# Moving the edge features' products of the last attention into the first four attention loops

## The chip, the cores and the metric

The kernel runs on one core of a Trainium2 chip. The core has five engines with a queue of instructions each: TensorE (PE: matrix products and transposes), VectorE (DVE), ScalarE (ACT), GpSimd (POOL) and SyncE (SP, which issues DMAs). Sixteen DMA engines move data between HBM and the on-chip memories. The metric is the time of one execution on the device, in microseconds; a shorter time is better.

## The reference

The program is a graph network on 3125 nodes with 256 numbers each and 50,000 edges, sorted by destination. Four attention layers over the edges alternate with four feed-forward layers, each added to x after a normalisation:

```
x = x + L0_gnn(norm(x))   # attention, 8 heads of 32
x = x + L0_ffn(norm(x))   # 16 experts, 2 per token
x = x + L1_gnn(norm(x))   # attention
x = x + L1_ffn(norm(x))   # 8 experts, 2 for the batch
x = x + L2_gnn(norm(x))   # two attentions, one after the other
x = x + L2_ffn(norm(x))   # an attention over 65,536 other edges gives the gates; 4 dense experts
x = x + L3_gnn(norm(x))   # attention with edge features
x = x + L3_ffn(norm(x))   # 8 dense experts
```

The last attention is the only one that uses the features of the edges, an input of 50,000 x 256 numbers:

```
e     = (edge_attr @ We).reshape(-1, 8, 32)
kj    = k[src] + e
alpha = sum(q[dst] * kj) / sqrt(32)          # then a softmax over the edges of one destination
out   = segment_sum((v[src] + e) * alpha)
```

The product `edge_attr @ We` depends on inputs alone, so it can be made at any time before the last attention. All arithmetic is in float32.

## The kernel before

The edges are laid out as 128 partitions of T = 391 consecutive edges; the last 48 places are padding. An attention runs over groups of GW = 8 columns of edges (8 x 128 edges), 49 groups in all. The stages follow each other: `gnn0`, `ffn0`, `gnn1`, `ffn1`, `gnn2` (two attentions, g2a and g2b), `ffn2`, `gnn3`, `ffn3`.

The first four attentions (g0, g1, g2a, g2b) share `gat_once`. One group is: eight gathers by GpSimd (`gather`, L129), each of which fetches 128 rows of 272 numbers into one of four buffers `hg`; the logits on VectorE (L607, L534); `weigh` (L624 on), where VectorE makes running maxima, ScalarE the exponential (L652) and a copy of the maxima (L653), and VectorE the weighted running sums (L660, L668); and a store of the group, 1088 KB, by SyncE (L611). TensorE has nothing to do in these loops, apart from the transposes of a sort (L338) which is laid into the first sixteen groups of g0. After the loop, `join_chunks` (L713) joins the chains that cross partitions. It begins with a gather of rows that were just stored (`fixrow`).

`ffn2` has a loop of its own, eight groups of GB = 64 gathers of 128 rows of 24 numbers (L1380). Into the first five groups it lays the 28 pieces of its experts' work on TensorE and ScalarE (`expert`, L1348; six pieces a group), whose results go to HBM in stores of 512 KB (L1370). In each of the eight groups it also calls `copy_features` (L952): one DMA that copies an eighth of the edge features, 6.2 MB, from the input to a second place in HBM called `attr`.

`gnn3` reads `attr`, never the input. When the given edges were not sorted, an `If` at its start (L838) fills `attr` in the order of the sort by gathers; with the given inputs this body is jumped over. The loop of gnn3 (L919) has 49 groups too, with sixteen gathers each: eight rows of 520 numbers (`kv`, three buffers) and eight rows of 256 (`q`). `project` (L894) runs two pairs of columns ahead of VectorE: it loads eight columns of `attr` (1 MB, L902), TensorE transposes a pair (L907, four transposes), ScalarE copies the result (L909), and TensorE multiplies it by We (L913). VectorE adds the product to k and v and multiplies by q (L930, L932, L933), sums over each head (L937) and goes on as in `weigh`.

In the attention loops and in that of ffn2 the order of VectorE and ScalarE is that of the program (`manual_schedule`). Elsewhere, and on the other engines, a scheduler orders the instructions when the program is built. Each engine works its queue in order.

Of the kernel before, what the change touches and what calls it, by code (L numbers as in the profile page):

```python
# [19 lines left out]
P = 128  # L20
# [18 lines left out]
class Kernel:  # L39
# [514 lines left out]
    def gat_once(self, L, tag, load_z, load_w, a_src, a_dst, H, dh, eps, loops, use):  # L554
# [11 lines left out]
        with tc.tile_pool(name=tag + "k", bufs=1) as kp:  # L566
# [25 lines left out]
            with tc.tile_pool(name=tag + "e", bufs=1) as sp, tc.tile_pool(name=tag + "v", bufs=4) as vp, \  # L592
# [7 lines left out]
                for t in range(0, T, GW):  # L600
# [10 lines left out]
                    nc.sync.dma_start(out=rows[:, t : t + n, :], in_=g[:, :n, :])  # L611
                nc.vector.tensor_copy(R, carry[0])
# [11 lines left out]
    def weigh(self, L, carry, vp, pp, t, n, l, g, H, dh):  # L624
# [32 lines left out]
        for j0 in range(0, n, GV):  # L657
            k = min(GV, n - j0)
            v = pp.tile([P, GV, W], F32, name="v")
# [167 lines left out]
    def gnn3(self, L):  # L827

        nc, tc, a, T, Ep = self.nc, self.tc, self.a, L.T, L.Ep
# [3 lines left out]
        Q = self.dram.tile([NP, C], F32, name="g3_Q")  # L833
        KV = self.dram.tile([NP, C + W], F32, name="g3_KV")
        OUT = self.dram.tile([Ep + 1 + P, RW], F32, name="g3_OUT")
        heads = lambda x: x.rearrange("p n (h d) -> p n h d", h=H)
        r = nc.values_load(L.wrong[0:1, 0:1], min_val=0, max_val=P)
        with tc.If(r > 0):  # L838
            with tc.tile_pool(name="g3s", bufs=3) as sp:
                rows = self.attr.rearrange("(p t) c -> p t c", p=P)  # L840
                for t in range(T):
                    x = sp.tile([P, C], F32, name="ax")
                    self.gather(x, a["edge_attr_256"], L.tab[:, t, 2:3])
                    nc.sync.dma_start(out=rows[:, t, :], in_=x)
# [37 lines left out]
        with tc.tile_pool(name="g3k", bufs=1) as kp:  # L882
            R = kp.tile([P, W], F32, name="R")
            mR = kp.tile([P, H], F32, name="mR")
            we = kp.tile([P, KC, C], F32, name="we")
            nc.sync.dma_start(out=we, in_=a["L3_gnn_We"].rearrange("(k p) f -> p k f", p=P))
            attr = self.attr.rearrange("(p t) c -> p t c", p=P)
            rows = OUT[:Ep].rearrange("(p t) w -> p t w", p=P)
            with tc.tile_pool(name="g3v", bufs=3) as vp, tc.tile_pool(name="g3vp", bufs=1, space=PSUM) as pp, \
# [4 lines left out]
                def project(i):  # L894
# [5 lines left out]
                    if j == 0:  # L900
                        at[t] = vp.tile([P, GW, C], F32, name="at", bufs=2)
                        nc.sync.dma_start(out=at[t][:, :n, :], in_=attr[:, t : t + n, :])  # L902
                    k2 = min(2, n - j)
                    pt = pp.tile([P, 2, KC, P], F32, name="apt")
# [6 lines left out]
                    for i2 in range(k2):  # L911
                        for k in range(KC):
                            nc.tensor.matmul(pe[:, i2, :], aT[:, i2, k, :], we[:, k, :], start=(k == 0), stop=(k == KC - 1))  # L913
                    proj[i] = pe

                project(0)
                project(1)
                carry, i = None, 0
                for t in range(0, T, GW):  # L919
# [6 lines left out]
                    for j in range(0, n, 2):  # L926
# [7 lines left out]
                        project(i + 2)  # L934
# [9 lines left out]
            self.join_chunks(L, "g3", OUT, R, mR, H, dh)  # L944
# [5 lines left out]
            self.node_results(L, "g3", OUT, H, dh, 1e-16, None, use)  # L950

    def copy_features(self, E, i, n):  # L952
# [596 lines left out]
```

## Time and profile before

| what | value |
|---|---|
| three timed runs | 7157.77, 7183.26 and 7185.37 us, median 7183.26 us |
| the profiled execution, its own time | 6277.97 us |
| its span, first to last instruction | 6275.9 us |
| mean granted clock of TensorE | 0.677 |
| busy shares of the span | PE 41%, DVE 56%, ACT 13%, POOL 51% |
| moved by DMA | 963.74 MB |
| loop of g0, first gather to last VectorE result | 148.4 to 666.1 us |
| loop of g1 | 1436.7 to 1940.5 us |
| loop of g2a | 2321.4 to 2824.7 us |
| loop of g2b | 2937.2 to 3438.7 us |
| loop of ffn2 | 3575.0 to 4342.8 us |
| loop of gnn3 | 4556.4 to 5577.2 us |

Times inside the program are microseconds from the start of the span. The profiled execution is shorter than the timed runs by some 900 us, and nothing on the page tells why; times of stages are of the profiled execution. A row of instructions reads: line, engine, operation, what it writes and reads, how often; then busy time and mean nanoseconds of one; then the idle time of the engine just before such instructions, with what ended most of it. "issue" is time in which an engine waited for nothing that the profile shows.

### The profile page before, as it was taken

What the parts mean: (1) busy time and instruction counts of PE and PEld (TensorE: products, weight loads), DVE (VectorE), ACT (ScalarE), POOL (GpSimd) and SP (SyncE); (2) the same over time, 40 slices, a digit from 0 to 9 for tenths busy, and PEclk for the clock granted to TensorE, in tenths of its full rate; (3) what the DMA queues carried; (4) which work ended last, traced back from release to release, by engine and by line L of the source; (5) the groups of instructions that cost most, each with busy time, mean ns of one, the idle gap of its engine ahead of it and who ended that gap; (6) DMA issues with size and microseconds to landing.
All of it is one profiled execution on the core that took longest, in us unless ns stands there. A gap on an engine that the chain in (4) does not pass through costs nothing. (4 is left out here: it accounts for less than half of the span.)

```text
span 6275.9 us, 39477 instructions
## 1 busy us (share of the span) xinstructions
PE 2584.4 (41%) x9265; PEld 1734.2 (28%) x9265; DVE 3504.1 (56%) x8011; ACT 794.9 (13%) x1810; POOL 3231.9 (51%) x3326
## 2 busy tenths in 40 slices
PE   2000049920001940002000499400566666639999
PEld 1000037710000530001000355200244555525555
DVE  6998611156886268884777411112778888871111
ACT  1000012210001110001000122100011111102222
POOL 3777430037774137775776576675077777730000
PEclk9555569955555975555555699755777666657999
DMA  5566335416663026663666234522377888730000
GB/s 193 191 225 221 124 115 169 156 57 197 223 219 109 14 64 224 220 218 109 212 212 204 52 109 123 154 55 67 144 256 262 264 268 262 264 123 16 10 11 26
DMA packets 398594, 963.74 MB, mean 154 GB/s; under 512 B 92478, under 2 KB 241053, under 8 KB 365966
## 3 DMA queue, kind: packets, MB, share of 16 engines
q1 hardware_dynamic: 236254, 538.71, 23.9%
q0 software_dynamic: 162096, 422.40, 23.2%
q8 instruction: 77, 1.26, 0.1%
q14 instruction: 167, 1.37, 0.1%
HBM read 611.38 MB, written 400.71 MB: 161 GB/s over the span
## 5 line engine op out<-in xcount | busy, mean ns | idle before, releaser
L724 PE MATMUL mRT<-ident,mR 128*8 128x128 f32 (+2 forms) x6 | 2.2, 372 | 2230.5 <-DVE mR L613 1356.0
L129 POOL DMA_INDIRECT hg<-g_H,A_tab x782 | 758.1, 969 | 240.4 <-issue 225.0
L668 DVE SCALAR_TENSOR_TENSOR hg<-hg,A_keep,v 128x264 f32<-128x264 f32 (+1 forms) x1368 | 666.2, 487 | 44.2
L129 POOL DMA_INDIRECT hg<-f_H,B_tab x512 | 519.3, 1014 | 232.9 <-issue 148.2
L724 PEld LDWEIGHTS mRT<-ident,mR 128*8 128x8 f32 (+2 forms) x6 | 0.5, 82 | 2233.1 <-issue 2233.1
L913 PE MATMUL ape<-we,aT 128*128 128x256 f32 x1564 | 493.6, 487 | 150.9 <-DVE kv L932 147.3
L129 POOL DMA_INDIRECT kv<-g_KV,A_tab x391 | 370.9, 949 | 295.3 <-issue 279.3
L660 DVE TENSOR_TENSOR v<-hg,e 128x1056 f32<-128x1056 f32 (+1 forms) x392 | 488.0, 1245 | 3.6 <-ACT e L652 3.6
L913 PEld LDWEIGHTS ape<-we,aT 128*128 128x128 f32 x1564 | 384.3, 252 | 251.1 <-DVE kv L932 164.4
L129 POOL DMA_INDIRECT hg<-g2a_H,A_tab x391 | 372.8, 953 | 119.2 <-issue 106.7
L129 POOL DMA_INDIRECT hg<-g2b_H,A_tab x391 | 371.5, 950 | 119.2 <-issue 114.0
L129 POOL DMA_INDIRECT q<-g_Q,A_tab x391 | 370.8, 948 | 120.1 <-issue 105.2
L1386 DVE TENSOR_TENSOR l<-hg,ad 128x256 f32<-128x256 f32 x8 | 6.3, 790 | 632.0 <-DMA hg<-f_H,B_tab 632.0
L1501 DVE SCALAR_TENSOR_TENSOR xs<-ps,g,xs 128x256 f32<-128x256 f32 x200 | 94.2, 484 | 458.1 <-PE ps L1500 458.1
L652 ACT ACTIVATE e<-d 128x72 f32<-128x72 f32 (+1 forms) x245 | 54.8, 223 | 2141.0 <-DVE d L649 2141.0
L125 PE MATMUL tr<-ident,z 128*128 128x128 f32 x450 | 109.5, 374 | 498.2 <-DVE z L117 434.6
L134 POOL DMA_INDIRECT A_Z<-D,A_first x100 | 99.3, 993 | 356.1 <-PE hps L584 223.4
L907 PE MATMUL apt<-ident,at 128*128 128x128 f32 x782 | 193.1, 382 | 196.6 <-ACT aT L909 188.2
L129 POOL DMA_INDIRECT y<-f_Y,pos x50 | 47.5, 949 | 398.3 <-DMA f_Y<-y 383.4
L125 PEld LDWEIGHTS tr<-ident,z 128*128 128x128 f32 x450 | 71.6, 200 | 535.1 <-ACT ln_rs L109 316.6
L1494 ACT ACTIVATE hT<-ps,bn 128x512 f32<-128x512 f32 (+1 forms) x224 | 162.4, 731 | 390.5 <-PE ps L1492 390.5
L930 DVE TENSOR_TENSOR kj<-kv,ape 128x512 f32<-128x512 f32 x196 | 135.9, 693 | 132.3 <-PE ape L913 112.1
(476 smaller groups left out, 6471.9 us busy)
## 6 DMA issues: line engine op xcount, KB each, us to landing
g_OUT<-hg SPq DMA_DIRECT2D x96, 1088.0 KB, 5.0
g2a_OUT<-hg SPq DMA_DIRECT2D x48, 1088.0 KB, 4.9
g_OUT<-kv SPq DMA_DIRECT2D x48, 1088.0 KB, 6.4
g2b_OUT<-hg SPq DMA_DIRECT2D x48, 1032.0 KB, 4.6
at<-attr SPq DMA_DIRECT2D x48, 1024.0 KB, 4.9
w<-in_L_ffn_w_dram SPq DMA_DIRECT2D x80, 512.0 KB, 3.9
attr<-in_edge_attr_dram SPq DMA_DIRECT2D x5, 6256.0 KB, 25.7
attr<-in_edge_attr_dram SPq DMA_DIRECT2D x3, 6240.0 KB, 26.9
```

Of the source, the lines that this page charges most:

```text
L125: nc.tensor.transpose(ps[:, k, :], z[:, t, k * P : (k + 1) * P], self.ident)
L129: return self.nc.gpsimd.indirect_dma_start(out=out, out_offset=None, in_=table, in_offset=bass.IndirectOffsetOnAxis(ap=idx, axis=0))
L134: i = self.nc.gpsimd.indirect_dma_start(out=table, out_offset=bass.IndirectOffsetOnAxis(ap=idx, axis=0), in_=in_, in_offset=None)
L652: nc.scalar.activation(e, d, AF.Exp)
L660: nc.vector.tensor_tensor(vals(v)[:, :k], vals(g[:, j0 : j0 + k, :W]), e[:, :, j0 + 1 : j0 + k + 1].rearrange("p h n -> p n h").unsqueeze( ...
L668: nc.vector.scalar_tensor_tensor(to, prev, L.keep[:, t + j0 + j : t + j0 + j + 1], v[:, j, :], op0=ALU.mult, op1=ALU.add)
L907: nc.tensor.transpose(pt[:, i2, k, :], at[t][:, j + i2, k * P : (k + 1) * P], self.ident)
L913: nc.tensor.matmul(pe[:, i2, :], aT[:, i2, k, :], we[:, k, :], start=(k == 0), stop=(k == KC - 1))
L930: nc.vector.tensor_tensor(kj[:, :k2], g[:, j : j + k2, :C], pe[:, :k2], ALU.add)
L1386: nc.vector.tensor_tensor(ln, g[:, :, W:].rearrange("p n h -> p h n"), ad[:, t : t + GB, :H].rearrange("p n h -> p h n"), ALU.add)
L1494: nc.scalar.activation(hT[:, f, :n], ps[:, :n], AF.Relu, bias=bn[l][1][:, c0 : c0 + 1], scale=bn[l][0][:, c0 : c0 + 1])
L1501: nc.vector.scalar_tensor_tensor(self.xs[:, t, :], po, g[:, t, e : e + 1], self.xs[:, t, :], op0=ALU.mult, op1=ALU.add)
```

## The change

The copy of the features is gone. Instead a new function `features` is called once in every group of the first four attention loops, 4 x 49 = 196 times, for a pair of columns each time. It is a pipeline of three steps, of which each call advances every pair in flight by one. One call copies the product of the pair before the last out of PSUM and stores it (256 KB to `attr`), copies the last pair's transposes out of PSUM and multiplies them by We, transposes a pair that was loaded at the call before, and loads the next pair (256 KB, two columns of each of the 128 partitions). `end_features` empties the pipeline after each loop. For the last 24 pairs, in g2b, where partition 127 has no edges left, a load is split into three or four DMAs. We is loaded once at the start and stays on chip. The tile `v` of `weigh` in PSUM has one buffer in place of two, to make room.

`attr` now holds products. In the last attention, `project` only loads eight columns and ScalarE copies them into PSUM, three pairs ahead; the transposes, copies and matrix products are gone. This goes for edges that came sorted, as here. For others the old way is kept, with gathers from the input in place of loads of `attr`. So the whole of `gnn3` is in the program twice, in the two arms of an `If`; the second arm is the one that runs here.

In ffn2, the experts' results are stored by two row blocks (256 KB, three buffers) and no longer by four (512 KB, two buffers).

```diff
                     carry = self.weigh(L, carry, vp, pp, t, n, l, g, H, dh)
                     nc.sync.dma_start(out=rows[:, t : t + n, :], in_=g[:, :n, :])
+                    self.features(vp, pp)
+                self.end_features(vp, pp)
...
-            v = pp.tile([P, GV, W], F32, name="v")
+            v = pp.tile([P, GV, W], F32, name="v", bufs=1)
...
+        r = self.nc.values_load(L.wrong[0:1, 0:1], min_val=0, max_val=P)
+        with self.tc.If(r > 0) as way:
+            self.gnn3_edges(L, False)
+        with way.Else():
+            self.gnn3_edges(L, True)
...
                     if j == 0:
                         at[t] = vp.tile([P, GW, C], F32, name="at", bufs=2)
-                        nc.sync.dma_start(out=at[t][:, :n, :], in_=attr[:, t : t + n, :])
+                        if ordered:
+                            nc.sync.dma_start(out=at[t][:, :n, :], in_=attr[:, t : t + n, :])
+                        else:
+                            for i2 in range(n):
+                                self.gather(at[t][:, i2, :], a["edge_attr_256"], L.tab[:, t + i2, 2:3])
                     k2 = min(2, n - j)
+                    if ordered:
+                        proj[i] = pp.tile([P, 2, C], F32, name="ape", bufs=3)
+                        nc.scalar.copy(proj[i][:, :k2], at[t][:, j : j + k2, :])
+                        return
...
+    def features(self, sp, pp, last=False):
+
+        nc, f = self.nc, self.feat
+        E, T = f["E"], f["T"]
...
+        loaded, turned, made = f["stages"]
+        if made is not None:
+            (t, n), pe = made
+            o = sp.tile([P, 2, C], F32, name="fe_o", bufs=2)
+            nc.scalar.copy(o[:, :n], pe[:, :n])
+            nc.sync.dma_start(out=rows[:, t : t + n, :], in_=o[:, :n])
+            made = None
+        if turned is not None:
+            (t, n), pt = turned
+            aT = sp.tile([P, 2, KC, P], F32, name="fe_T", bufs=2)
+            nc.scalar.copy(aT[:, :n], pt[:, :n])
+            pe = pp.tile([P, 2, C], F32, name="fe_p", bufs=1)
+            for i in range(n):
+                for k in range(KC):
+                    nc.tensor.matmul(pe[:, i, :], aT[:, i, k, :], self.feat_we[:, k, :], start=(k == 0), stop=(k == KC - 1))
+            made, turned = ((t, n), pe), None
+        if loaded is not None:
+            (t, n), at = loaded
+            pt = pp.tile([P, 2, KC, P], F32, name="fe_t", bufs=1)
+            for i in range(n):
+                for k in range(KC):
+                    nc.tensor.transpose(pt[:, i, k, :], at[:, i, k * P : (k + 1) * P], self.ident)
+            turned, loaded = ((t, n), pt), None
+        if not last and f["at"] < len(f["units"]):
+            t, n = f["units"][f["at"]]
+            f["at"] += 1
+            at = sp.tile([P, 2, C], F32, name="fe_a", bufs=3)
+            if full * T + t + n <= E:
+                whole = bass.AP(tensor=src.tensor, offset=src.offset + t * C, ap=[[T * C, P], [1, n * C]])
+                nc.sync.dma_start(out=at[:, :n, :].rearrange("p n c -> p (n c)"), in_=whole)
...
-                    y = wp.tile([P, 4, C], F32, name="y")
                     for i in range(n // P):
+                        if i % 2 == 0:
+                            y = wp.tile([P, 2, C], F32, name="y", bufs=3)
...
-                    self.copy_features(50000, i, T // GB)
```

## The prediction

> **What bounds the kernel now.** The page's busy shares name no bound: GpSimd 51%, VectorE 56%, TensorE 41%. So I cut the span at the loops and read busy time by stage; the rows below are g1, g2a, ffn2 and gnn3 (columns: stretch, its length, busy time of each engine, granted clock, DMA share, GB/s).
>
> ```profile
> 1438.00:1945.00 507.00, 1.80 (x5) 0.87 (x5) 406.12 (x850) 27.55 (x100) 373.38 (x392) 0.50 0.65 218
> 2321.00:2830.00 509.00, 1.97 (x5) 0.86 (x5) 406.55 (x850) 27.54 (x100) 374.72 (x394) 0.50 0.65 217
> 3575.00:4343.00 768.00, 412.48 (x1403) 244.63 (x1401) 113.31 (x247) 118.74 (x223) 519.30 (x512) 0.77 0.37 105
> 4556.00:5577.00 1021.00, 665.39 (x2346) 510.53 (x2346) 853.74 (x1372) 134.12 (x295) 741.69 (x782) 0.68 0.77 256
> ```
>
> In gnn3 VectorE looks like the bound (854 of 1021 us) and TensorE like the second. The groups of gathers say otherwise:
>
> ```profile
> L129 POOL DMA_INDIRECT hg<-f_H,B_tab x512 | 519.3, 1014 | 232.9 <-issue 148.2 <-DMA hg<-f_H,B_tab 84.7
> L129 POOL DMA_INDIRECT kv<-g_KV,A_tab x391 | 370.9, 949 | 295.3 <-issue 279.3 <-DMA kv<-g_KV,A_tab 4.3 <-DVE acc L656 3.7
> L129 POOL DMA_INDIRECT q<-g_Q,A_tab x391 | 370.8, 948 | 120.1 <-issue 105.2 <-DMA q<-g_Q,A_tab 4.9 <-DVE kv L668 2.1
> L129 POOL DMA_INDIRECT hg<-g2a_H,A_tab x391 | 372.8, 953 | 119.2 <-issue 106.7 <-DVE hg L668 12.5
> ```
>
> A gather takes 0.95 us, 0.30 us of issue precedes it, and it waits for next to nothing: 1.254 us from start to start. In gnn3 782 x 1.254 = 981 us, and from the first gather to the last there are 984. In g1, g2a, g2b 391 x 1.254 = 490 against 492 to 493. So GpSimd's issue sets all these loops; VectorE, TensorE and the DMAs run beneath it. Only ffn2 is off its floor: 512 x 1.254 = 642, and it takes 752. The timeline of GpSimd and SyncE there (start, duration, instruction, idle time before) shows why:
>
> ```profile
> 4042.17 3.44 POOL L129 DMA_INDIRECT hg<-f_H,B_tab  x1 [0.30 <-issue]
> ...
> 4052.51 0.56 SPq L960 DMA_DIRECT2D attr<-in_edge_attr_dram  x1
> ...
> 4064.40 0.95 POOL L129 DMA_INDIRECT hg<-f_H,B_tab  x1 [2.18 <-DMA hg<-f_H,B_tab]
> 4070.73 0.95 POOL L129 DMA_INDIRECT hg<-f_H,B_tab  x1 [5.38 <-DMA hg<-f_H,B_tab]
> 4076.65 0.94 POOL L129 DMA_INDIRECT hg<-f_H,B_tab  x1 [4.97 <-DMA hg<-f_H,B_tab]
> 4078.68 0.94 POOL L129 DMA_INDIRECT hg<-f_H,B_tab  x1 [1.08 <-DMA hg<-f_H,B_tab]
> ```
>
> After each copy of features (26 us to land) gathers wait for earlier gathers that are stuck behind it. A second loss is of another kind: some gathers are long themselves (3.44 us at 4042).
>
> **The change part by part**, against the profiled execution (6277.97 us).
>
> *The copy goes: -77 us.* The DMA waits are 84.7 us over 26 gathers, of which 26 x 0.3 is the usual issue: 77 remain, about 9.6 for each of eight copies. The long gathers stay. Of the whole excess of 110 us one would hope to get 110; [...] the 3.44 us gather lies under VectorE's 3.35 us multiply (L1405), the 2.40 us one under the 1.77 us copy (L1415). [...] I take 77, with 60 to 110 as ends. What could cover the gain: the experts. Six pieces take about 93 us of TensorE (28 in 435 us), a group of gathers would take 64 x 1.254 + 4 = 84. But the experts end with the fifth group at 3993, where the gathers of that group would then end too (3575 + 82 + 4 x 84.6 = 3995), and three buffers `hg` let GpSimd run ahead. So nothing is lost, barely. The smaller stores of y (256 KB) have 100 half-pieces of ScalarE to hide under: nothing.
>
> *The last attention's TensorE work goes: -24 us, all at its end.* 1564 matrix products of 487 ns, 782 transposes of 382 and 196 copies of 583 leave, and 196 copies from SBUF of the same shape come, some 0.58 us each, beneath VectorE. In the loop this is worth nothing: it lies under the 981 us of GpSimd. But VectorE, with 18 us of work and some 2 us of waits for `ape` in each 20 us, lags, and works off its last groups when the gathers are over:
>
> ```profile
> 5532.03 0.95 POOL L129 DMA_INDIRECT kv<-g_KV,A_tab  x1 [3.74 <-DVE acc L656]
> ...
> 5539.55 0.95 POOL L129 DMA_INDIRECT kv<-g_KV,A_tab  x1 [0.31 <-issue]
> ...
> 5543.50 0.70 DVE L930 TENSOR_TENSOR kj<-kv,ape 128x512 f32<-128x512 f32 x1 [1.30 <-PE ape L913]
> ...
> 5565.95 0.43 DVE L930 TENSOR_TENSOR kj<-kv,ape 128x256 f32<-128x256 f32 x1
> ...
> 5577.03 0.16 DVE L942 COPY mR<-m 128x8 f32<-128x8 f32 x1
> ```
>
> Without the waits VectorE (18.2 us) keeps up with GpSimd (20.06). The last gather lands 4.2 us after 5539.55, and from the last pair to mR there are 11.2 us: the end is at 5555 and not 5577, -22, and the 3.4 us wait at 5532 goes: I take -24 (-10 to -27). The bound itself is untouched.
>
> *gnn3 in an arm of an If: +7 us.* Before, the jump cost VectorE 1.02 us, over a body that held nothing for it. At the first If of the program VectorE jumps over some 1300 instructions:
>
> ```profile
> 41.04 0.42 DVE L191 CAST dstf<-A_tab 128x391 f32<-128x391 int32 x1 [4.28 <-DVEq L189]
> 4444.57 0.28 DVE L856 MEMSET none_row<- 1x272 f32 x1 [1.02 <-issue]
> ```
>
> The new jump is over as many, and the normalisation behind it is on the path. [...] by the nearer-looking row (1.02) the sum would gain nothing here, [...] I take 3.3. At the arm's end nothing of ffn3 can be ordered into gnn3's tail any more; before, the statistics of six of 25 tiles were (0.4 us each), [...] so +4 (0 to 10).
>
> *The features in four loops: +12 us.* Each group of 10.03 us gets four transposes (1.5 us by L907's row) and eight products (3.9 by L913's), on a TensorE that has 1.8 us of work in 507; two ScalarE copies of 0.58 on an engine with 27.5 us of work, placed after `weigh`, when VectorE has 6.6 us of sums to go; no instruction for VectorE or GpSimd. All that is hidden; if the cover were gone it would be the two copies in front of an exponential, 1.2 us a group. SyncE gets a load and a store a group, 512 KB: 196 x 512 KB = 100 MB, just the bytes of the copy that goes. A loop's rate rises by 25.7 MB / 507 us = 51 GB/s, from 218 to 269. The nearest row is gnn3, whose loop runs at 256 GB/s (the page's slices: up to 268): its 782 gathers wait 9.2 us for DMA in all, so 4.6 for 391. Four loops: 0 to 18, I take 8. The loads stand two groups ahead in SyncE's order, so they wait for nothing of their own group. The last pairs drain after the loop: a copy, four products and a copy, some 5 us after the last exponential, while `fixrow` waits 4.1 us for the last store anyway: 1 us a loop, +4 (0 to 12).
>
> *The sort in g0: +10 us.* In its first 16 groups VectorE is busy 175 of 185 us, and the sort's transposes now queue on TensorE behind the features' products, up to 4 us for each of 14. Slack after that doesn't come back, since GpSimd cannot catch up. 0 to 40; I take 10, near the bottom, since VectorE has the loop's own work between two steps of the sort. `v` with one buffer is written and read by VectorE alone, in order: nothing.
>
> Sum: -77 - 24 + 3 + 4 + 8 + 4 + 10 = -72 us, 6278 to 6206.
>
> **Against the median.** The timed runs are 7183 / 6278 = 1.144 times the profiled execution, and no row tells where the 905 us lie. If they lie outside the stages touched, the change is worth 72; if all is stretched alike, 82. I take 82: 7183 - 82 = 7101, forecast **7100 us** (its own range 7050 to 7145).
>
> **Rivals.**
> *The wait moves with the bytes.* The copy cost 77 us for 51 MB read and written. If a byte costs a gather as much in the four loops as in ffn2, 100 MB of loads and stores give 77 back, and with the 24 us of the tail and the 29 of other costs the sum is about +5: 7183 +- 25. For it: in ffn2 GpSimd stops some ten gathers after a burst. Against it: the group's own store of 1088 KB lands in 5.0 us without one DMA wait in g2a's row, and 256 KB more twice is a burst of some 2 us, not of 26.
> *The loops become bound by the stores, slower.* SyncE's queue and the 16 DMA engines have to pass 512 KB more in each 10.03 us; if `hg` comes free later than GpSimd needs it, each of 196 groups stretches. The row has the beginning of such a wait (12.5 us for `hg` in g2a). At 0.37 us a group the gain is used up, at 1 us it is +196 - 80 = +116, times 1.144: 7315. Against it: the DMA share of 0.65 would become about 0.8, which gnn3 bears.
> *gnn3's loop gets faster too*, if something other than issue sets the 1.254 us: its VectorE and TensorE suggest it, the row of waits speaks against it. 40 us more: 7055.
>
> **How the numbers follow.** The forecast 0.60, the bytes 0.20, the stores 0.13, the faster loop 0.07. Range 7035 to 7195: the low end is 110 for the copy and 26 for the tail, scaled; the high end has the sort at +40, the loops at +30 and half of the first gain. Half a percent (36 us) is about what a measurement of this kernel can tell from no change. Faster: 0.60 + 0.07 + a small part of the bytes, 0.68; same 0.19; slower 0.13.
>
> **What would show it.** Right: in ffn2 no gather waits for a DMA, and the loop takes about 690 us; gnn3's gathers still take 981 us, and mR follows the last one by about 15 us, not 37; the loops of g1 to g2b take 504 to 510 us. Wrong: DMA or `hg` waits in the rows of g1 to g2b, a g0 loop of over 550 us, or VectorE waiting over 5 us at the start of gnn3.

## The result and the profile after

The changed kernel takes 7232 us (15 runs, 7208 to 7250) against 7180 us for the kernel before in the same session (15 runs, 7158 to 7207): ratio 1.0067, 95% interval 1.0050 to 1.0084, so it is slower by two thirds of a percent. The forecast was 7100 us. The same program has two lengths, by session. The kernel before takes 6273 to 6282 us in four of the sessions below and 7124 to 7180 us in the other three and in that of the result; the profile shown before the prediction is of the first kind, its three timed runs of the second. They are called short and long sessions here. A session is a stretch of runs on one chip, with the kernel before and its variants in turn; comparisons are made within a session, or the text says that they are not.

The profile of the changed kernel is of the long kind (7250 us, span 7248.3). Its rows by stage, for g1, g2a, ffn2 and gnn3 (stretch, its length, busy time of PE, PEld, DVE, ACT, POOL, granted clock, DMA share, GB/s):

```profile
1571.00:2197.00 626.00, 196.45 (x571) 147.27 (x570) 406.12 (x844) 74.50 (x194) 372.66 (x392) 0.60 0.64 215
2580.00:3215.00 635.00, 199.22 (x570) 148.82 (x569) 406.22 (x844) 74.73 (x194) 373.76 (x393) 0.60 0.63 212
4094.00:5133.00 1039.00, 485.17 (x1434) 274.44 (x1432) 110.62 (x247) 120.59 (x226) 495.09 (x513) 0.70 0.12 28
5350.00:6547.00 1197.00, 0.37 (x1) 0.08 (x1) 859.89 (x1373) 142.17 (x295) 739.17 (x782) 0.50 0.66 218
```

The loops take 626 and 635 us where 507 and 509 were read before, with the same busy time of VectorE and GpSimd: all of the difference is idle. The groups of gathers say what GpSimd waited for:

```profile
L129 POOL DMA_INDIRECT hg<-f_H,B_tab x512 | 494.7, 966 | 527.8 <-DMA f_OUT<-hg 284.6 <-issue 243.2
L129 POOL DMA_INDIRECT q<-g3o_Q,A_tab x391 | 369.6, 945 | 289.4 <-DVE l L640 173.5 <-issue 114.1 <-DMA kv<-g3o_KV,A_tab 0.9
L129 POOL DMA_INDIRECT hg<-g2a_H,A_tab x391 | 372.4, 952 | 232.3 <-issue 114.5 <-DVE hg L670 32.6 <-DVE acc L658 24.4
```

A gather still takes 0.95 us, but in g2a it idles 232 us and not 119, and the new part is waits for a buffer `hg`, which the profile puts down to VectorE's sums. GpSimd's issue no longer sets these loops.

The changed kernel's trace of a short session (span 6191.2 us) has the same instructions, stage by stage:

```profile
1447.00:1952.00 505.00, 211.25 (x572) 157.21 (x573) 409.20 (x844) 71.15 (x194) 373.52 (x393) 0.60 0.81 266
2329.00:2834.00 505.00, 209.80 (x566) 156.40 (x567) 409.21 (x844) 71.26 (x194) 373.60 (x393) 0.61 0.80 265
3585.00:4271.00 686.00, 419.32 (x1429) 249.25 (x1428) 112.71 (x247) 120.72 (x226) 514.34 (x512) 0.81 0.21 43
4486.00:5489.00 1003.00, 0.37 (x1) 0.08 (x1) 854.72 (x1373) 142.16 (x295) 739.49 (x782) 0.50 0.81 260
```

These are the stages as forecast: 505, 686 (about 690 was said) and 1003; the DMA share of g1 is 0.81, where about 0.8 was said. So there are two questions: whether the steps of the sum hold where the profile was taken, and what they turn into in a long session.

All stages in one table; each is the time from the first gather to the copy into mR, from the traces named; "loops" is the sum of g0, g1, g2a and g2b, "rest" all that lies outside the six stages. "y in pieces" and "two arms" are runs of the next section.

| kernel (session: time of the kernel before) | loops | ffn2 | gnn3 | rest | span |
|---|---|---|---|---|---|
| before (short, 6273) | 2024.1 | 767.5 | 1021.1 | 2463.1 | 6275.8 |
| changed (short, 6282) | 2031.5 | 686.0 | 1002.1 | 2471.6 | 6191.2 |
| before with y in pieces (long, 7124) | 2309.6 | 1046.6 | 1250.0 | 2492.1 | 7098.3 |
| changed (long, 7167) | 2488.5 | 1041.5 | 1182.4 | 2515.6 | 7228.0 |
| two arms, no features array (long, 7167) | 2323.4 | 1032.5 | 1278.0 | 2507.9 | 7141.8 |

Between the first and the third row lie 822 us, of which 793 are in the six stages with gathers and 29 in the rest: that is where the 905 us are that "no row tells".

### The profile page after: what moved, and what is told of

It is laid out like the page before. It is cut to its first block, busy times and chain, and to the rows that moved or that the text cites. A ratio compares the mean times of both kernels' runs of the same rounds, so it can differ in the third digit from the quotient of the medians.

```text
span 7248.3 us, 40809 instructions
## 1 busy us (share of the span) xinstructions
PE 2813.8 (39%) x9265; PEld 1865.6 (26%) x9265; DVE 3518.2 (49%) x8011; ACT 996.4 (14%) x2202; POOL 3201.0 (44%) x3326
## 5 line engine op out<-in xcount | busy, mean ns | idle before, releaser
L993 PE MATMUL fe_p<-feat_we,fe_T 128*128 128x256 f32 x1564 | 683.9, 613 | 1610.6 <-ACT fe_T L989 890.8
L993 PEld LDWEIGHTS fe_p<-feat_we,fe_T 128*128 128x128 f32 x1564 | 464.7, 311 | 1769.1 <-ACT fe_T L989 926.4
L129 POOL DMA_INDIRECT hg<-f_H,B_tab x512 | 494.7, 966 | 527.8 <-DMA f_OUT<-hg 284.6
L129 POOL DMA_INDIRECT kv<-g3o_KV,A_tab x391 | 369.6, 945 | 310.3 <-DMA g3o_KV<-qkv 176.8
L129 POOL DMA_INDIRECT q<-g3o_Q,A_tab x391 | 369.6, 945 | 289.4 <-DVE l L640 173.5
L1466 DVE TENSOR_TENSOR v<-hg,l 128x1280 f32<-128x1280 f32 x8 | 26.7, 3340 | 782.3 <-ACT l L1463 781.8
L1420 PE MATMUL ps<-zT,w 128*128 128x512 f32 (+1 forms) x448 | 209.0, 611 | 304.6 <-ACT hT L1421 158.7
L1427 PE MATMUL ps<-w,hT 128*128 128x256 f32 x800 | 229.8, 433 | 130.5 <-ACT hT L1421 75.3
L911 ACT COPY ape<-at 128x512 f32<-128x512 f32 x196 | 115.2, 588 | 904.3 <-DVE q L943 356.3
```

The costliest lines, as they stand in the source:

```text
L129: return self.nc.gpsimd.indirect_dma_start(out=out, out_offset=None, in_=table, in_offset=bass.IndirectOffsetOnAxis(ap=idx, axis=0))
L911: nc.scalar.copy(proj[i][:, :k2], at[t][:, j : j + k2, :])
L993: nc.tensor.matmul(pe[:, i, :], aT[:, i, k, :], self.feat_we[:, k, :], start=(k == 0), stop=(k == KC - 1))
L1420: nc.tensor.matmul(ps[:, :n], w1[:, k, f * P : (f + 1) * P], zT[:, k, b0 : b0 + n], start=(k == 0), stop=(k == KC - 1))
L1427: nc.tensor.matmul(po, hT[:, f, i * P : (i + 1) * P], w2[:, f, :], start=(f == 0), stop=False)
```

## The experiments

**The kernel before once more.** No edit.

> The kernel before, profiled once more, since its first profile (6278 us) is of an execution 900 us shorter than its timed ones and the changed kernel's profile (7250 us) is not. Theory A (the 900 us lie in the gather loops, which in the timed executions are no longer held by GpSimd's issue of 1.254 us a gather): a profile of about 7180 us with the loops of g0 to g2b at 560 to 620 us each in place of 502 to 518, ffn2 at 950 to 1040 in place of 768, gnn3 at 1150 to 1200 in place of 1021. Theory B (the 900 us lie outside the stages that the change touches): these loops within 15 us of the first profile. Time 7180, ratio 1.000.

Measured: 6273.6 us, ratio 1.0002 (0.9993 to 1.0011), every stage within 1 us of the first profile. The session was a short one, so neither theory was tested; it showed that the first profile was no stray execution.

**Two kernels without the copy, rows straight from the input.** The first is the changed kernel without its features in the loops, the second the kernel before without its copy:

```
-                    self.features(vp, pp)                     # first kernel only
-                self.end_features(vp, pp)                     # first kernel only
-                    self.copy_features(50000, i, T // GB)     # second kernel only
-    nc.sync.dma_start(out=at[t][:, :n, :], in_=attr[:, t : t + n, :])
+    nc.sync.dma_start(out=at[t][:127, :n, :], in_=whole[:, t : t + n, :])
+    nc.sync.dma_start(out=at[t][127:, :k, :], in_=...)        # the last partition
```

> The changed kernel without its features in the four loops: no loads, transposes, products and stores there, and the last attention loads its rows straight from the input, so that the products are left out of the result. Theory A (the features' work in the loops costs more than the 12 + 10 us forecast, because the loops are not held by GpSimd there): 60 to 200 us below the changed kernel, about 7030 to 7170. Theory B (the loops carry the features for nothing, the loss is in ffn2 or in gnn3): within 30 us of the changed kernel, 7200 to 7260.

> The kernel before without the copy of features in ffn2; the last attention loads its rows straight from the input and still makes the products. Theory A (ffn2 is held by the experts in the timed executions, so the copy costs little): 7165 to 7185, ratio 0.998 to 1.001. Theory B (the copy costs the forecast 77 us, or 88 scaled): 7090 to 7110, ratio 0.988 to 0.990.

Measured: 7739 and 7731 us in a short session, ratios 1.234 and 1.232; both theories of each missed. gnn3 took 2555 us and more, because of the way the loads were cut: in the second kernel's trace the two loads of a group (name, count, duration in ns: smallest, median, largest) held SyncE like this,

```profile
L905 SPq DMA_DIRECT2D at<-in_edge_attr_dram x4: 4339/20962/21482, 4902.8 to 5057.3; - x4
L907 SPq DMA_DIRECT2D at<-in_edge_attr_dram x4: 23227/28963/29530, 4923.9 to 5078.8; - x4
```

21 and 29 us to issue, where a load over 128 partitions takes 0.33 us on the same line of the later kernel of this form. So the two times say nothing of the features; ffn2 can be read, 689 us each against 767, 78 us for the copy.

**The changed kernel, and parts of it, in one short session.** First the changed kernel itself.

> The changed kernel once more, beside the kernel before on the same chip. The kernel before took 6273 us on the chip of the first experiments and 7180 on that of the result, with the same instructions. Theory A (the steps of the forecast hold where the loops are held by GpSimd's issue, and fail where they are not): if the kernel before takes about 6273 here, 6195 to 6215, ratio 0.988 to 0.991, with g1 to g2b at 502 to 510 us, ffn2 at 680 to 690 and gnn3 at 990 to 1000; if it takes about 7180, ratio 1.005 to 1.008. Theory B (the features cost the loops wherever the kernel runs): ratio 1.004 to 1.010 in both, g1 to g2b over 515 us.

Measured: 6206.4 us against 6282.3, ratio 0.9881 (0.9864 to 0.9897): 76 us less, where the forecast's sum had 72. Theory A holds here, and B falls: g1 to g2b are 503.5, 503.8 and 499.9 us.

Then the kernel before without the copy, with loads over all 128 partitions:

```
-    nc.sync.dma_start(out=at[t][:, :n, :], in_=attr[:, t : t + n, :])
+    whole = bass.AP(tensor=src.tensor, offset=src.offset + t * C, ap=[[T * C, P], [1, n * C]])
+    nc.sync.dma_start(out=at[t][:, :n, :].rearrange("p n c -> p (n c)"), in_=whole)
```

> The kernel before without the copy of features in ffn2; the last attention loads its rows straight from the input, all 128 partitions in one transfer, and still makes the products there. The run whose loads took 127 partitions and then one lost 1458 us in gnn3, so that its ffn2 alone can be read (82 us shorter). Theory A (the copy's removal is worth the forecast 77 us where GpSimd's issue holds ffn2): 6185 to 6200 where the kernel before takes 6273, ratio 0.986 to 0.989; where it takes 7180, ratio 0.998 to 1.001. Theory B (the loads from the input cost gnn3 what ffn2 wins): ratio 0.998 to 1.005.

Measured: 6202.0 us, ratio 0.9871 (0.9854 to 0.9887); ffn2 689.5, gnn3 1019.9. Theory B falls; by the ratio A holds, though the time lies 2 us over its interval. The copy alone was worth the 78 us, and everything else that the change does came to about nothing there.

Then the features added to the kernel before, with `v` in one buffer and `y` in pieces as in the changed kernel (with the larger `y` the pool of ffn2 needs 40 KB of a partition, and 39.7 are left there). The lines in the loops:

```
                     nc.sync.dma_start(out=rows[:, t : t + n, :], in_=g[:, :n, :])
+                    self.features(vp, pp)
+                self.end_features(vp, pp)
```

> The kernel before with the features' loads, products and stores added in the first four loops, the stores going to an array that nobody reads; v in one buffer and y in pieces of two blocks, as in the changed kernel; the copy and the last attention stay as they are. Theory A (they cost 12 + 10 us where GpSimd's issue holds the loops): 6285 to 6305 where the kernel before takes 6273, ratio 1.002 to 1.005; where it takes 7180, 7240 to 7350, ratio 1.008 to 1.024. Theory B (they cost the loops wherever the kernel runs): ratio over 1.008 in both.

Measured: 6293.0 us, ratio 1.0020 (1.0013 to 1.0027): +11 us, where +22 was forecast for loops and sort; at the low edge of theory A.

And the changed kernel without them:

> The changed kernel without its features in the four loops; the last attention loads its rows straight from the input, all 128 partitions in one transfer, and copies them, so that the products are left out of the result. Theory A: 6273 - 77 - 24 + 7 = 6180 (6170 to 6195) where the kernel before takes 6273, ratio 0.984 to 0.988; where it takes 7180, ratio 0.980 to 0.997, and below the changed kernel by 60 us or more. Theory B (the loss is in ffn2 or gnn3, not in the loops): within 30 us of the changed kernel.

Measured: 6197.6 us, ratio 0.9864 (0.9847 to 0.9880), 9 us below the changed kernel, as theory A has it within its interval; B cannot be told from it here.

**v in one buffer** (kernel before, `bufs=1` for `v`).

> The kernel before with v in one buffer and nothing else changed. Theory A (the forecast's step: v is written and read by VectorE alone, in order): no change, ratio 0.999 to 1.001, and every gather loop within 2 us of the kernel before. Theory B (the next multiply into v has to wait for the last sums of the one before): 0.1 us or more for each of some 980 multiplies, ratio over 1.008. Where the kernel before takes about 7180 us, its profile also tells by stage where the 900 us lie: theory C, that they lie in the gather loops alone and grow with what is recorded in them, has the loops of g1 to g2b at under 610 us, below the changed kernel's 612 to 634, and gnn3 at over 1180.

Measured: 6278.6 us, ratio 1.0004 (0.9995 to 1.0013), short session. It costs nothing that can be measured, as theory A has it.

**y in pieces** (kernel before, stores of two blocks from three buffers). This run was on the same chip as the one before, seven minutes later, and the session was a long one: it is not the chip.

> The kernel before with y stored in pieces of two blocks from three buffers, and nothing else changed. Theory A (the forecast's step: the smaller stores are hidden): ratio 0.999 to 1.001, ffn2 from its first gather to mR 767 us, as before. Theory B (24 stores more in SyncE's queue, each ahead of the copy of its group, delay the copies or the output stores): ffn2 longer by 3 to 10 us. Where the kernel before takes about 7180 us, its profile tells by stage where the 900 us lie; theory C as in the run with v in one buffer.

Measured: 7121.5 against 7124.4 us, ratio 1.0002 (0.9988 to 1.0016): the smaller stores cost nothing that can be measured, as theory A has it. With this ratio its trace stands for the kernel before in a long session:

```profile
1510.00:2093.00 583.00, 0.37 (x1) 0.08 (x1) 401.45 (x846) 27.36 (x99) 373.21 (x392) 0.50 0.57 189
2477.00:3062.00 585.00, 0.75 (x3) 0.36 (x3) 402.25 (x848) 27.38 (x99) 373.02 (x392) 0.50 0.57 189
3768.00:4817.00 1049.00, 529.15 (x1599) 310.70 (x1599) 161.45 (x414) 137.77 (x285) 484.26 (x500) 0.70 0.24 65
5029.00:6281.00 1252.00, 743.93 (x2394) 530.98 (x2394) 835.63 (x1426) 135.97 (x296) 690.36 (x731) 0.70 0.60 202
```

Its loops are not at GpSimd's 490 us either, but 44 to 51 us below those of the result's profile (another long session); its ffn2 is as long as the changed kernel's although the copy is in it. Theory C's times hold for the loops and for gnn3 (583 and 585 us for under 610, 1252 for over 1180); that they grow with what is recorded in them is not shown by that.

**Transfers alone, engines' work alone, neither.** Three kernels in one long session (the kernel before 7167.0 us). In the first, the rows are stored as they were loaded; in the second, transposes, products and copies work on fixed rows, with no load or store; the third has no features in the loops.

```
 first:   made, turned, loaded = turned, loaded, None     # no transposes, products, copies
 second:  loaded = (t, n), self.feat_we                   # in place of the loaded rows
          # and no dma_start in features()
```

> The changed kernel with only the transfers of its features in the four loops: each group loads its 256 KB and stores them, as loaded, three groups later; no transposes, products and copies there, so that the products are left out of the result. Where the kernel before takes about 7150 us, the four loops of the changed kernel are 44 to 51 us longer each than those of the kernel before. Theory D (the transfers make that, by what is recorded of them or by their traffic): loops of g1 to g2b at 610 to 635 us, ratio 1.004 to 1.010, as the changed kernel. Theory I (the 14 instructions of TensorE and ScalarE in each group make it): loops at 567 to 585, ratio 0.978 to 0.985. Both by half: loops at 590 to 605, ratio 0.990 to 0.998. Where the kernel before takes about 6275: ratio 0.986 to 0.989 by each.

> The changed kernel with only the transposes, products and copies of its features in the four loops, on fixed rows (the weights), without a load or a store in the loops; the last attention loads its rows from the input, so that the products are left out of the result. Where the kernel before takes about 7150 us: theory D, loops of g1 to g2b at 567 to 585 us, ratio 0.978 to 0.985; theory I, 610 to 635 us, ratio 1.004 to 1.010; both by half, 590 to 605, ratio 0.990 to 0.998. Where it takes about 6275: ratio 0.985 to 0.989 by each.

> The changed kernel without its features in the four loops, on the same chip as the two before; the last attention loads its rows straight from the input and copies them, so that the products are left out of the result. Where the kernel before takes about 7150 us: the loops' part of the loss goes, 189 us less than the changed kernel by the stages of the traces, ratio 0.978 to 0.985, and ffn2 stays at 1030 to 1050, as the copy's removal is worth 9 us there. If ratio is over 0.995, the features are not what the changed kernel lost by. Where it takes about 6275: 0.985 to 0.989, as before.

Measured: 7085.1 (0.9888, 0.9858 to 0.9917), 7107.4 (0.9911, 0.9887 to 0.9934) and 7057.2 us (0.9840, 0.9812 to 0.9869). The sums of the four loops are 2347.1, 2377.5 and 2342.0 us: transfers cost 5 us, the work of the engines 36. The last is as expected. D falls, and I explains a part at most. The ratios lie within or just below the interval of "both by half", but two halves should make up the whole: the changed kernel's loops are 2488 us in another session of the same length (below), so some 105 us come only with the two together, which no theory here had.

**Loads without stores, stores without loads, and two arms.** In one long session (the kernel before 7166.8 us), with the changed kernel beside them.

> The changed kernel, beside the three that follow. Where the kernel before takes about 7150 us: ratio 1.004 to 1.010, four loops of 600 to 640 us each. Where it takes about 6275: ratio 0.986 to 0.990.

> The changed kernel with the features' loads, transposes, products and copies in the four loops but without their stores; the last attention loads its rows from the input, so that the products are left out of the result. Where the kernel before takes about 7150 us: theory L (the loads feeding the transposes make the excess of the two together), four loops within 25 us of the changed kernel's sum, ratio 1.002 to 1.010; theory S (the stores fed by the copies make it), four loops 80 to 120 us below the changed kernel's sum, ratio 0.987 to 0.994; theory E (no pairing, each instruction and record in these loops has its price, growing with their number), in the middle, ratio 0.995 to 1.001. Where it takes about 6275: 0.985 to 0.990 by each.

> The changed kernel with the features' transposes, products, copies and stores in the four loops, made from fixed rows (the weights) without a load in the loops, so that the products of the edges are left out of the result. Where the kernel before takes about 7150 us: theory L, four loops 80 to 120 us below the changed kernel's sum, ratio 0.987 to 0.994; theory S, within 25 us of it, ratio 1.002 to 1.010; theory E, in the middle, ratio 0.995 to 1.001. Where it takes about 6275: 0.985 to 0.990 by each.

> The kernel before without the copy and without the array of features: the last attention has two arms, one that loads its rows straight from the input for sorted edges and one that gathers them for others, and makes the products itself. Where the kernel before takes about 7150 us: ffn2 9 us shorter and the rest as before, 0.996 to 1.001 and below the changed kernel by 0.5 to 1%. Where it takes about 6275: 6195 to 6210, ratio 0.987 to 0.990, within 10 us of the changed kernel. Against that: the If's arm could cost more than 7 us here, since TensorE's instructions stand in it.

Measured: the changed kernel 7233.9 us (1.0102, 1.0078 to 1.0126), without stores 7201.4 (1.0049, 1.0022 to 1.0076), without loads 7116.8 (0.9943, 0.9922 to 0.9963), two arms 7153.4 (0.9980, 0.9969 to 0.9990). The loops are 2488.5, 2468.7, 2380.1 and 2323.4 us. Theory L is right: the excess stays without the stores (20 us less in the loops) and goes with the loads (108 us less, for 80 to 120 expected). The last kernel is the kernel before without the array of features, with loads over all 128 partitions as above in one arm of the If; in the same session it is 0.2% faster than the kernel before and 1.1% faster than the changed one.

What a load does is in SyncE's queue. Waits of that queue during g1 (line of the waiting instruction, what it waited for, us in total, times, longest), in the changed kernel's long profile, where L1008 is the load and L611 the loop's own store of g:

```profile
SPq L1008 <- remote: 218.4, 18, 21.8
SPq L1008 <- PE fe_t L1000: 59.4, 19, 5.1
```

and in the kernel without loads, in its g1:

```profile
SPq L984 <- ACT fe_o L983: 118.8, 36, 6.6
SPq L611 <- DVE l L607: 101.9, 17, 9.8
SPq L611 <- DVE hg L670: 53.6, 10, 12.3
```

The load waits for the signal that the transposes have given its buffer back, up to 22 us ("remote" is a release whose sender the trace doesn't tell; the load's only wait there is for TensorE); without it the store waits for VectorE alone, which is its proper wait. One such place of the changed kernel, SyncE, VectorE, GpSimd, then TensorE and ScalarE (start, duration, instruction, idle time before):

```profile
1741.93 0.33 SPq L1008 DMA_DIRECT2D fe_a<-in_edge_attr_dram  x1
1742.61 0.32 SPq L611 DMA_DIRECT2D g_OUT<-hg  x1
1743.03 0.37 SPq L984 DMA_DIRECT2D attr<-fe_o  x1
1747.24 0.33 SPq L1008 DMA_DIRECT2D fe_a<-in_edge_attr_dram  x1
1747.92 0.32 SPq L611 DMA_DIRECT2D g_OUT<-hg  x1
```

```profile
1717.98 2.06 DVE L670 SCALAR_TENSOR_TENSOR hg<-hg,A_keep,v 128x264 f32<-128x264 f32 x4
...
1730.03 0.49 DVE L670 SCALAR_TENSOR_TENSOR hg<-acc,A_keep,v 128x264 f32<-128x264 f32 x1 [1.57 <-remote]
1731.43 0.49 DVE L670 SCALAR_TENSOR_TENSOR hg<-hg,A_keep,v 128x264 f32<-128x264 f32 x1 [0.91 <-DVE hg L670]
1732.15 0.49 DVE L670 SCALAR_TENSOR_TENSOR hg<-hg,A_keep,v 128x264 f32<-128x264 f32 x1 [0.22 <-DVE hg L670]
1733.55 0.49 DVE L670 SCALAR_TENSOR_TENSOR hg<-hg,A_keep,v 128x264 f32<-128x264 f32 x1 [0.91 <-issue]
```

```profile
1735.54 0.95 POOL L129 DMA_INDIRECT hg<-g_H,A_tab  x1 [0.30 <-issue]
1749.33 0.94 POOL L129 DMA_INDIRECT hg<-g_H,A_tab  x1 [12.84 <-DVE hg L670]
```

```profile
1717.72 0.60 PE L1000 MATMUL fe_t<-ident,fe_a 128*128 128x128 f32 x4
```

```profile
1741.94 0.58 ACT L989 COPY fe_T<-fe_t 128x512 f32<-128x512 f32 x1 [8.52 <-remote]
```

A group's last sum ends at 1720.04, but its store leaves at 1742.61, right behind a load; GpSimd, three buffers on, stands still for 12.84 us. The transposes that the load waits for end at 1718.32 by the trace, yet the load leaves only at 1741.93, and ScalarE's copy of these transposes at 1741.94. Over the 196 groups of the four loops the store leaves this much after the last sum (mean, and number of groups over 5 us): changed kernel 6.6 us, 79; without stores 6.0, 76; transfers alone 1.2, 21; without loads 0.2, none; engines' work alone 0.3, none; no features 0.3, none. GpSimd's stops of over 5 us in the loops sum to 402 us, 422, 164, 237, 238 and 150 in the same order. All 38 of these stops of the changed kernel stand before the first gather of a group, and before 37 of them the store of the group four earlier, whose buffer is the one to be filled, had left over 5 us late. In 37 of the 147 groups of g0, g1 and g2a of the result's profile the load left over 5 us after the transposes had ended by the trace and SyncE was free; some 610 of the 1015 us that the loads wait in these three loops lie there. The ends of matrix products are modelled in these traces, so they can't tell transposes that end late from a signal that comes late. A pair's rows are loaded 32 us ahead of its transposes on the mean, so late rows are not it.

In the short session the load waits as well, and is just covered. SyncE there, then VectorE:

```profile
1596.08 0.32 SPq L984 DMA_DIRECT2D attr<-fe_o  x1
1600.87 0.33 SPq L1008 DMA_DIRECT2D fe_a<-in_edge_attr_dram  x1
1602.39 0.32 SPq L611 DMA_DIRECT2D g_OUT<-hg  x1
```

```profile
1600.30 2.06 DVE L670 SCALAR_TENSOR_TENSOR hg<-hg,A_keep,v 128x264 f32<-128x264 f32 x4
```

The load stands ahead of the store of its group in SyncE's order, is held for 4.5 us, and leaves at 1601.20; the store is due at 1602.36. The cover is 1.2 us here; over the groups of g0, g1 and g2a it is 0.8 us in the median and never under 0.4, and no store is held up.

**The loads, then loads and stores, issued by ScalarE**, behind the copy that has waited for the same transposes anyway:

```
-                nc.sync.dma_start(out=at[:, :n, :].rearrange("p n c -> p (n c)"), in_=whole)
+                nc.scalar.dma_start(out=at[:, :n, :].rearrange("p n c -> p (n c)"), in_=whole)
```

> The changed kernel with the features' loads issued by ScalarE instead of SyncE, each right behind the copy of transposed rows that has waited for the transposes which free its buffer; the stores stay on SyncE. Where the kernel before takes about 7150 us: theory Q (in SyncE's queue the load's wait for a transpose holds up the store of g behind it), the store of g goes out within 1.5 us of the last sum on the mean in place of 6 to 6.6, the four loops fall from 2488 to between 2370 and 2410 us, ratio 0.993 to 0.998, below both kernels. Theory R (late rows hold up TensorE and ScalarE): loops at 2460 to 2500 us, ratio 1.004 to 1.011. Where it takes about 6275: 0.986 to 0.990 by each.

> As the run before, and the features' stores issued by ScalarE too, each right behind the copy that fills it, so that SyncE has the loop's stores of g alone. Where the kernel before takes about 7150 us: theory Q, delay of the store of g 0.2 to 0.4 us, loops at 2360 to 2400 us, ratio 0.992 to 0.997. Theory R: 2460 to 2500 us, ratio 1.004 to 1.011. Where it takes about 6275: 0.986 to 0.990.

Measured: 6198.4 (0.9876, 0.9856 to 0.9895) and 6193.8 us (0.9873, 0.9854 to 0.9893) against 6273.2. The session was a short one, where both theories say the same, so the remedy was not tested where it matters. That the load's place in SyncE's queue makes the excess thus rests on the traces and on the kernels with one of the two parts left out: loads that wait for no transposes cost 5 us, transposes without loads 36, both together 146. That moving the load away cures it was not shown.

## Why the prediction was wrong

*Against the median* is where it failed as a whole: "If they lie outside the stages touched, the change is worth 72; if all is stretched alike, 82." The 905 us lie in the stages touched, and not as an even lengthening of all: the engines lag there at intervals, and the loops have another bound. A sum made against a profile that is 905 us away from the timed runs had to say what each step costs where GpSimd's issue does not set the loops; it did so for none.

*The features in four loops: +12 us* is the step that turned the sign. "The loads stand two groups ahead in SyncE's order, so they wait for nothing of their own group" is false in both kinds of session: placed ahead of its group's store, a load waits for that group's transposes. The short session covers it by about a microsecond, and there the step held: ffn2 starts 10.5 us later for features and sort together (22 forecast), of which g0 has 6.3. In the long session the loops are 165 us longer than those of the two-arm kernel (2488.5 against 2323.4), where the step and that of the sort had 22; some 105 of it is the load with its transposes, 36 the engines' work, 5 the transfers, each by the sums above. The remaining 19 us lie between two kernels without features, of different sessions, and so are the uncertainty of such sums.

*The copy goes: -77 us* is right in mechanism and size in the short session: ffn2 767.5 to 686.0, -81.5. No gather waits for a DMA there any more:

```profile
L129 POOL DMA_INDIRECT hg<-f_H,B_tab x512 | 514.3, 1005 | 156.0 <-issue 155.7 <-DMA hg<-f_H,B_tab 0.3
```

The long gathers stayed, as the forecast had it: 1005 ns on the mean after, 1014 before. That their excess, (1014-950) x 512 = 33 us, would not go with the copy was the author's estimate; what makes them long no run here shows. In the profile before, all 25 gathers of ffn2 over 1.1 us overlap an instruction of VectorE, the 14 over 2 us the multiplies of L1405 (seven) and the copies of L1415 (seven), and the 452 that overlap none take 0.94 to 0.96 us. In the long sessions the copy is worth some 5 to 17 us (1046.6 with it, 1029.3 to 1041.5 without, in other sessions). The cover that the step named and dismissed, "So nothing is lost, barely", decides there: the 28 pieces take 928 us from the first product to the last, and not 432, so that six of them outlast the 80 us of a group of gathers. TensorE in ffn2 of the changed kernel's long profile, and what VectorE waits for in that stage there:

```profile
4500.03 1.01 PE L1420 MATMUL ps<-zT,w 128*128 128x512 f32 x1 [1.79 <-issue]
4502.83 1.01 PE L1420 MATMUL ps<-zT,w 128*128 128x512 f32 x1 [1.79 <-issue]
4505.63 1.01 PE L1420 MATMUL ps<-zT,w 128*128 128x512 f32 x1 [1.79 <-issue]
```

```profile
DVE v L1466 <- ACT l L1463: 781.8, 7, 231.7
```

One product in 2.80 us, ready but not issued; the exponentials l stand on ScalarE behind the experts' copies. In the short session that wait is 89.9 us in all.

*The last attention's TensorE work: -24 us.* Short: gnn3 is 19 us shorter. The gathers end after 979.3 us, 5 less, and from there to mR it is 22.8 us and not 36.7; the forecast had the place right and 15 us for that rest. Long: 68 to 96 us (1182.4 against 1250.0 and 1278.0), so that "in the loop this is worth nothing" is wrong there. It is the third rival, for another reason than forecast, since the loop there is not set by GpSimd's issue; and it pays back over a third of what the loops lose.

*gnn3 in an arm: +7 us.* Its two parts were measured in the short session almost to the number: VectorE reaches its first instruction in the arm after 4.33 us, not 1.02,

```profile
4377.02 0.28 DVE L859 MEMSET none_row<- 1x272 f32 x1 [4.33 <-issue]
```

close to the 4.28 of the jump at the program's first If: 3.31 us more than before, for 4.28 - 1.02 = 3.3. That this row would hold and not the nearer-looking one was the author's estimate. What follows gnn3 is 4.1 us longer (703.1 against 699.0), for +4, of which 2.4 was the statistics and the rest an estimate that no run takes apart.

*The sum.* In the short session the spans differ by 84.6 us and the medians by 76, for 72 forecast; in the long ones it is +52 (the result) and +67 (the later session). Against the two-arm kernel of the later session, whose trace was taken beside it, the spans differ by +86: +165 in the loops, -96 in gnn3, +9 in ffn2 and +8 in the rest.

*The rivals.* "The wait moves with the bytes" falls: all the bytes without the engines' work cost 5 us. "The loops become bound by the stores, slower" is the one that came true in kind: `hg` comes free later, 165 us over 196 groups is 0.84 us a group, and 1 us was put there. Its reason was wrong, since the DMA share of g1 is 0.64, no higher than in the first profile (0.65): it is the place in the queue, not the load on it. The things named to show the forecast wrong (a g0 loop of over 550 us, `hg` waits in g1 to g2b, VectorE waiting at the start of gnn3) are in part what the profile has: g0 is 628 us, and `hg` waits appear in each loop. Both also hold for the kernel before in a long session (g0 579 us), so they tell of the session as much as of the change. VectorE's wait at the start of gnn3, 11.6 us for the first gathers, is no longer than before (12.4).

## What to carry to other kernels

In this kernel a load that fills a recycled buffer waited in SyncE's queue for the transposes that free that buffer, up to 21.8 us, and the store behind it waited too (6.6 us after the last sum on the mean, 0.2 without loads). Before putting such a load ahead of a store that frees buffers for the bound engine, work out by how many microseconds it is covered: the 0.8 us of cover in the short session (the median) did not last in the long one. When a profile's own time is far from the timed runs, do not scale the sum: ask which stages the difference lies in, and price each step also for a loop whose bound has moved. The array of features was not needed at all: reading the input over all 128 partitions gives the whole gain of the change in a short session (6202.0 us, the changed kernel 6206.4) and, with two arms, stays below both kernels in a long one (7153.4 us against 7166.8 and 7233.9).

## What the runs showed of the hardware

*Stretches in which nothing is issued for long.* The two traces of the changed kernel have the same 40,809 instructions, of nearly equal durations, and 1057 us between their spans. 1013 of it lie in the six stages with gathers and 44 in the rest; behind gnn3 the two run alike (703.1 and 701.9 us). In each loop of the long trace some ten stretches of about 23 us appear, one in about 52 us. In them VectorE's instructions start a multiple of about 0.70 us apart, as at 1731.43, 1732.15 and 1733.55 above, each ready before, and what waits for TensorE's transposes leaves late, as at 1741.93; gathers keep their 1.25 us (1733.04, 1734.29, 1735.54) until buffers run out. The kernels whose loads feed transposes had 40 to 42 such stretches in the four loops, the others some 30 to 35, one in about 60 us; whether late stores lead to more stretches or more stretches to late stores, no run here separates.

What makes them is not settled. That the recording of the execution does is a guess of the author's, and one thing speaks for it: the long trace holds 31,188 semaphore events and the short one of the same program 85,177, most of those missing are in the stages with gathers (g1 has 3.6 a microsecond in the long trace and 19 in the short one), and the events that are left come some 0.7 us apart in the stretches, as the instructions start. At 19 events a microsecond, the 30 us between two stretches are some 570 events; for the kernel before, at the 15.7 a microsecond of g1 in its short trace and 38 us, they are some 600 (estimates from these numbers, which take the rates of short sessions). So by events the stretches lie about as far apart in the one kernel as in the other. Why one session has them and the next on the same chip not, and whether a run without recording would have them, no run here shows.

*A load over 127 partitions.* It held the issuing queue for 21 us, and the one-partition load behind it for 29, against 0.33 us over 128, and gnn3 was some 1535 us longer (2555 against 1019.9). Of the load's packets of 8 KB at most two ran at once in that trace, where up to 19 did over 128 partitions. Why, no run here shows.
